# Two Toeplitz products summed in DRAM by the storing DMA, and a gate that loads and transposes one tensor instead of two

## The chip, the core and the metric

The kernel runs on one core of one Trainium2 chip. The core has five engines with queues of their own: TensorE (PE in the profile; its weight loads are shown apart as PEld), VectorE (DVE), ScalarE (ACT), GpSimd (POOL) and SyncE (SP), which here only issues transfers. Transfers issued by SP and by GpSimd run on the same 16 DMA engines. On-chip memory is SBUF (128 partitions) and PSUM ([...]into which TensorE writes its products); DRAM holds everything that doesn't fit. The metric is the time of one execution on the device, in microseconds (us).

## The reference, cut to what matters

The model is four layers on x of shape (8, 56, 56, 192): a Toeplitz gate, window attention, a depthwise convolution and a four-direction selective scan, with group or layer norms and residual sums between them. The change concerns the first layer only:

```python
p = silu(x @ p_w.T + p_b)                      # 576 channels
q = silu(x @ q_w.T + q_b)
v = silu(x @ v_w.T + v_b)
qv = q * v
o1 = toeplitz(qv along w, a1)                  # for every row h: a 56 x 56 Toeplitz matrix per channel
o2 = toeplitz(qv along h, a2)                  # for every column w: another one per channel
out = (p * (o1 + o2)) @ o_w.T + o_b
```

`a1` and `a2` come from small networks over the positions, once for all images. The sum `o1 + o2` is formed for each of 8 x 3136 tokens and 576 channels, all in float32.

## The kernel before, in words

**Order of the stages.** A first stage makes `qv` of images 0 to 3 (`products`) and writes it to DRAM as `qv_d[b][block]`, six blocks of 96 channels, tokens in rows of 96 values (384 bytes). The second makes both Toeplitz products of those images (`toeplitz`). Then the front of image 0 (gate, attention, convolution, inner projections, step sizes) runs step by step beside `products` and `toeplitz` of images 4 to 7. Last comes the scan loop over 5376 steps ("pairs": a chunk of 448 tokens, 128 channels and two states), 672 an image; into it the front of the next image is woven by a planner.

**`toeplitz`.** For each axis (the variable `ax`; 0 is the product along h, 1 the one along w) and each block of 96 channels: eight loads of 588 KB (two halves `u` of the other direction x four images) bring `qv` into `x` (tile `tzx`, L261), with 56 partitions for the position in the sequence in each half, and the other direction and the channels in the free one. On axis 0 a partition is a row h, and its 28 tokens of an image lie in one run of 28 x 384 bytes in DRAM; on axis 1 a partition is a column w, and each run has 384 bytes. Then for each of four groups of 24 channels, two loads (L270) place a Toeplitz matrix for each channel twice on the diagonal of `tm` (three buffers), TensorE makes one 112 x 112 x 112 product a channel (L274; each float32 product leaves two records in the profile), and VectorE and ScalarE copy four channels at a time from PSUM back over `x` (L280; VectorE alone in the second run). At the end of a block, eight stores on GpSimd's queue (L288) write `x` to `o_d[ax][b]`. Axis 1 is stored in the order (w, h), which makes its runs long; so the two products lie in DRAM in different token orders. `x` has three buffers in the first run and two in the second.

**The gate** (`gate`, one image): for each of seven chunks of 448 tokens, six projections (L467) with their bias (L471), one SiLU over them all (L473), then for each of six channel blocks one PSUM bank (L484): four groups of 112 tokens, and in each two products with the identity matrix, of the product along h and of that along w, that turn tokens x channels into channels x tokens and add the two in PSUM. VectorE multiplies `p` by the bank (L492). Two output products of six each follow (L497), a residual sum (L503) and statistics (L504). `load_ot` fetches two blocks at a time, one step ahead: for each block one load of the product along h (L444) and two of that along w (L450), which put its tokens back into the order (h, w); six transfers in all.

**What sets the order.** Every engine takes its queue in the order of the program. In the scan loop a step is: GpSimd fills the ring (L1007), ScalarE the decays (L1024), VectorE scans (L1033), GpSimd or VectorE in turn multiplies by C (L1039, tile `hc`, four buffers), TensorE sums with identity products (L1054). Between the steps, the planner (`Parts`) places pieces of the next image's front. A piece ends at each `yield`; `Meter` prices the pieces while the front of image 0 is emitted (0.04 us + 1.25 ns an element for a product), and a piece is placed when by these prices it fits into the engines' spare time. A front holds at most two PSUM banks (`ps`). In the second stage, pieces of `products` and `toeplitz` of images 4 to 7 are drawn after each piece of the front, 1.0 of the planner's us for every four channels, in the ratio of 0.55 to the price of the front's piece.

Of the kernel before, what the change touches and what calls it, by code (L numbers as in the profile page):

```python
# [15 lines left out]
F32 = mybir.dt.float32  # L16
AF = mybir.ActivationFunctionType
ALU = mybir.AluOpType
# [4 lines left out]
H = W = 56  # L23
L = H * W
C = 192
CP = 96
D1 = 576
CH = 448
NCH = L // CH
TT = 112  # L30
# [54 lines left out]
def model(ctx: ExitStack, tc: tile.TileContext, a: dict, out: bass.AP):  # L85
    nc = tc.nc
    B = out.shape[0]
# [8 lines left out]
    ident = load_const(const, "ident")  # L96
# [6 lines left out]
    ext = [dram.tile([D1 // TC, TT, TC], F32, name=f"ext{i}") for i in range(2)]  # L103

    qv_d = [dram.tile([D1 // CP, L, CP], F32, name=f"qv{b}") for b in range(B)]
    o_d = [[dram.tile([D1 // CP, L, CP], F32, name=f"o{i}_{b}") for b in range(B)] for i in range(2)]
    x1_d, x2_d, x3_d = ([dram.tile([C, L], F32, name=f"x{i}_{b}") for b in range(B)] for i in (1, 2, 3))
    z_d = [dram.tile([128, ND, L], F32, name=f"z{b}") for b in range(B)]
    zr_d = [dram.tile([128, ND, L], F32, name=f"zr{b}") for b in range(B)]
# [129 lines left out]
    def toeplitz(images, beside):  # L239
        G = len(images) * (H // 2)  # L240
        with (
            tc.tile_pool(name="tz", bufs=2) as sp,
            tc.tile_pool(name="tz_t", bufs=1) as tp,
            tc.tile_pool(name="tz_ps", bufs=4 if beside else 8, space=PSUM) as ps,
        ):

            tm = [tp.tile([TT, TT, TC], F32, name=f"tm{i}") for i in range(3)]
            for t in tm:
                nc.gpsimd.memset(t, 0.0)
            n_t = 0  # L250
            for ax in range(2):
                along_h = "(h u w) c -> u h w c"
                along_w = "(u h w) c -> u w h c"
                stored = "(w u h) c -> u w h c"
                size = dict(h=H, u=2) if ax == 0 else dict(w=W, u=2)
                for c0 in range(D1 // CP):
                    x = sp.tile([TT, G, CP], F32, name="tzx", bufs=2 if beside else 3)
                    for n, b in enumerate(images):
                        v = qv_d[b][c0].rearrange(along_w if ax else along_h, **size)
                        for u in range(2):  # L260
                            nc.sync.dma_start(out=x[u * W : (u + 1) * W, n * 28 : (n + 1) * 28, :], in_=v[u])  # L261
                    for c1 in range(0, CP, TC):
                        t = tm[n_t % 3]
                        n_t += 1
                        e = ext[1 - ax][(c0 * CP + c1) // TC]

                        src = bass.AP(e.tensor, e.offset, [[TC, W], [1, W * TC]])
                        for u in range(2):
                            dst = t[u * W : (u + 1) * W, u * W : (u + 1) * W, :].rearrange("p i c -> p (i c)")
                            nc.sync.dma_start(out=dst, in_=src)  # L270
                        for c2 in range(0, TC, 4):
# [8 lines left out]
                            copy(  # L280
                                x[:, :, cs].rearrange("p (b g) c -> p b g c", g=28)[:, :, ::-1, :],
                                po.rearrange("p c (b g) -> p b g c", g=28),
                            )
                            yield 1.0
                    for n, b in enumerate(images):
                        v = o_d[ax][b][c0].rearrange(stored if ax else along_h, **size)
                        for u in range(2):
                            nc.gpsimd.dma_start(out=v[1 - u], in_=x[u * W : (u + 1) * W, n * 28 : (n + 1) * 28, :])  # L288


    now, later = range(min(4, B)), range(min(4, B), B)
# [5 lines left out]
    with (  # L297
# [17 lines left out]
        def carve(base, parts, *shapes):  # L315

            views, at = [], 0
            for shape in shapes:
                n = 1
                for m in shape:  # L320
                    n *= m
                v = base[:parts, at : at + n]
                if len(shape) > 1:
                    names = [f"a{i}" for i in range(len(shape))]
                    v = v.rearrange(
                        f"p ({' '.join(names)}) -> p {' '.join(names)}", **dict(zip(names[1:], shape[1:]))
                    )
# [101 lines left out]

        def gate(b):  # L430

            w_p, w_o, x, s, ot = carve(slab, TT, (2, D1), (6, C), (2, 2, CH), (6, CH), (2, 2, 4, C))
# [21 lines left out]

            load_x(0)
            load_ot(0)
# [2 lines left out]
            for j in range(NCH):  # L459
# [15 lines left out]
                for c in range(6):  # L475
                    n = 3 * j + c // 2
                    if c % 2 == 0 and n + 1 < 3 * NCH:
                        load_ot(n + 1)
                    yield 0, 1

                    p = bank()
                    for t in range(4):
                        for i in range(2):
                            nc.tensor.matmul(  # L484
                                p[:CP, t * TT : (t + 1) * TT],
                                ot[:, n % 2, i, t, c % 2 * CP : c % 2 * CP + CP],
                                ident[:TT, :TT],
                                start=i == 0,
                                stop=i == 1,
                            )  # L490
                    yield 1, 0
                    nc.vector.tensor_mul(s[:, c, :], s[:, c, :], p[:CP, :CH])  # L492
                for m in range(2):
# [876 lines left out]
```

## Time and profile before

Three runs took 21826.98, 21839.35 and 21850.64 us; the median is 21839.35. The profiled execution took 21800.17 us, with a span of 21798.4 us from its first to its last instruction and a mean granted TensorE clock of 0.888.

| engine | busy us | share of the span |
|---|---|---|
| TensorE | 18274.4 | 84% |
| VectorE | 15858.5 | 73% |
| GpSimd | 15084.9 | 69% |
| ScalarE | 12098.2 | 56% |

| what (line) | count | busy us | mean of one |
|---|---|---|---|
| Toeplitz products (L274), records | 4608 | 1031.5 | 403 ns |
| gate's identity products (L484), records in the scan loop | 4704 | 522.4 | 265 ns |
| attention's transposes (L647), records in the scan loop | 1344 | 336.5 | 326 ns |
| gate's multiplication (L492) in the scan loop | 294 | 177.2 | 603 ns |
| product stores (L288) issued by GpSimd | 192 | 97.3 | 513 ns |
| gate's loads of the product along h (L444), 168 KB each | 336 | | |
| gate's loads of the product along w (L450), 84 KB each | 672 | | |

A share is an average over stages with different limits, so the stretch that an edit touches has to be looked at by itself. Records of one operation overlap: TensorE's 403 ns is from start to end, while the next one starts sooner. The span falls into `products` (to 505 us), `toeplitz` of images 0 to 3 (505 to 1120), the front of image 0 beside the products of images 4 to 7 (to about 3355), and the scan loop. In the first front, whose instructions were emitted through the pricing helper, lines of the front appear as L79.

### The profile page before, as it was taken

Reading aid. Unit: us, or ns where it says so; the run is one execution under the profiler, and the core shown is the slowest. Engines: PE = TensorE matmul, PEld = TensorE weight load, DVE = VectorE, ACT = ScalarE, POOL = GpSimd, SP = SyncE. Lnnn points to the kernel's source line nnn. Section 1 sums busy time; section 2 is a strip of 40 time slices with the busy share of each in tenths; the row PEclk is TensorE's granted clock in tenths of the full one; section 3 lists DMA queues with packets and bytes.
Section 4 is the critical chain, followed back from the end, with each engine's and each line's share of the span. In section 5 each row is a group of like instructions: output and inputs, shape, how many; then the busy total and the mean of one; then the engine's idle time right before and its main releaser. Section 6 shows DMA issues by size and latency. Waiting matters only on the chain. (4 is left out here: it accounts for less than half of the span.)

```text
span 21798.4 us, 194536 instructions
## 1 busy us (share of the span) xinstructions
PE 18274.4 (84%) x58396; PEld 9706.4 (45%) x58396; DVE 15858.5 (73%) x12604; ACT 12098.2 (56%) x28153; POOL 15084.9 (69%) x9175
## 2 busy tenths in 40 slices
PE   7978977888888989888888889888988888887777
PEld 4845654444443434444444434443444444343333
DVE  2122117996799768986799769976898589976998
ACT  3126114655666466755666566746675566656555
POOL 0000006887789778977788768976898678877998
PEclk9588868999999989998999989998999899998888
DMA  3931575444544455445644455345544464445443
GB/s 86 245 98 49 170 196 169 126 135 159 187 143 135 136 184 170 129 129 171 184 133 136 154 184 150 123 150 170 169 129 140 156 185 132 135 155 175 134 138 116
DMA packets 2419572, 3249.82 MB, mean 149 GB/s; under 512 B 917598, under 2 KB 2361024, under 8 KB 2387554
## 3 DMA queue, kind: packets, MB, share of 16 engines
q1 hardware_dynamic: 2398292, 3121.12, 47.5%
q0 software_dynamic: 15520, 116.14, 1.4%
q8 instruction: 463, 7.59, 0.1%
q14 instruction: 593, 4.86, 0.1%
q10 hardware_dynamic: 4704, 0.12, 0.0%
HBM read 2661.35 MB, written 575.48 MB: 148 GB/s over the span
## 5 line engine op out<-in xcount | busy, mean ns | idle before, releaser
L1007 POOL TENSOR_TENSOR ring<-du,bm 128x896 f32<-128x896 f32 x5376 | 9447.8, 1771 | 1983.9 <-ACT ring L1014 1937.8
L1054 PE MATMUL ps_y<-hc,ident_sb 128*128 128x448 f32 x21504 | 9818.6, 591 | 590.2 <-POOL hc L1039 573.3
L1024 ACT ACTIVATE ps_a<-delta,A_logs_sb 128x449 f32<-128x449 f32 x10752 | 6858.4, 638 | 331.5 <-DVE ring L1033 68.7
L1054 PEld LDWEIGHTS ps_y<-hc,ident_sb 128*128 128x128 f32 x21504 | 4271.5, 207 | 4640.8 <-issue 3494.9
L1033 DVE TENSOR_TENSOR_SCAN ps_a<-ps_a,ring 128x898 f32<-128x898 f32 x2688 | 5429.0, 2020 | 1062.5 <-ACT ring L1014 555.0
L1033 DVE TENSOR_TENSOR_SCAN ring<-ps_a,ring 128x898 f32<-128x898 f32 x2688 | 5423.0, 2017 | 420.4 <-ACT state L1046 177.3
L1039 POOL TENSOR_TENSOR hc<-ring,cm 128x896 f32<-128x896 f32 x2688 | 4758.0, 1770 | 860.9 <-DVE ring L1033 349.3
L1039 DVE TENSOR_TENSOR hc<-ps_a,cm 128x896 f32<-128x896 f32 x2688 | 2935.0, 1092 | 974.5 <-PE ps_y L1054 753.3
L1046 ACT COPY state<-ps_a 128x2 f32<-128x2 f32 x2687 | 425.3, 158 | 3254.0 <-DVE hc L1039 3250.0
L280 DVE COPY tzx<-ps_tz 112x448 f32<-112x448 f32 x432 | 269.8, 625 | 1389.9 <-PE ps_tz L274 1175.0
L274 PE MATMUL ps_tz<-tzx,tm 112*112 112x112 f32 x4608 | 1031.5, 403 | 257.6 <-DMA tm<-ext 233.0
L288 POOL DMA_DIRECT2D o<-tzx x192 | 97.3, 513 | 1653.6 <-DVE tzx L280 1318.7
L274 PEld LDWEIGHTS ps_tz<-tzx,tm 112*112 112x112 f32 x4608 | 1028.0, 319 | 295.2 <-issue 288.7
L817 PE MATMUL ps_f<-slab 128*128 128x448 f32 x2646 | 1086.4, 546 | 69.9 <-DMA slab<-dg_d 62.1
L1046 ACT COPY state<-ring 128x2 f32<-128x2 f32 x2688 | 504.9, 188 | 791.3 <-DVE ring L1033 778.4
L647 PE MATMUL ps_f<-ident_sb,slab 98*98 98x98 f32 x1344 | 336.5, 326 | 619.6 <-ACT slab L640 619.6
L749 PE MATMUL ps_f<-slab 96*96 96x448 f32 x1764 | 725.1, 547 | 47.7 <-DVE slab L736 47.7
L817 PEld LDWEIGHTS ps_f<-slab 128*128 128x128 f32 x2646 | 506.8, 192 | 560.5 <-issue 485.0
L79 PE MATMUL ps_f<-slab 96*96 96x448 f32 (+6 forms) x2306 | 731.2, 497 | 10.2 <-DMA slab<-x 4.9
L990 POOL TENSOR_TENSOR du<-delta,xcd 128x448 f32<-128x448 f32 x672 | 658.6, 980 | 23.6 <-DMA xcd<-xc 23.6
L647 PEld LDWEIGHTS ps_f<-ident_sb,slab 98*98 98x98 f32 x1344 | 203.9, 158 | 1033.7 <-ACT slab L640 814.6
L227 PE MATMUL ps_qv<-wqv,xn 96*128 96x384 f32 (+1 forms) x1200 | 527.0, 522 | 128.2 <-DVE xn L146 67.5
(218 smaller groups left out, 17070.7 us busy)
## 6 DMA issues: line engine op xcount, KB each, us to landing
bm<-bc SPq DMA_DIRECT2D x1792, 448.0 KB
cm<-bc SPq DMA_DIRECT2D x1792, 448.0 KB
xcd<-xc SPq DMA_DIRECT2D x840, 224.0 KB
dl<-slab SPq DMA_DIRECT2D x224, 672.0 KB
delta<-dl SPq DMA_DIRECT2D x224, 672.0 KB
tzx<-qv SPq DMA_DIRECT2D x192, 588.0 KB
o<-tzx POOLq DMA_DIRECT2D x192, 588.0 KB, 13.7
slab<-x SPq DMA_DIRECT2D x224, 336.0 KB
```

What stands on the lines that cost most here:

```text
L79: return f(*args, **kw)
L274: nc.tensor.matmul(po[:, c, :], t[:, :, c2 + c], x[:, :, c1 + c2 + c], start=True, stop=True)
L647: nc.tensor.transpose(p[:PT_, e * PT_ : (e + 1) * PT_], S[:, 3 * g + e, :], ident[:PT_, :PT_])
L749: nc.tensor.matmul(p[:CP, :CH], dg[:, k, t, :], xp[:, u, k, dy : dy + 8, dx : dx + W], start=t == 0, stop=t == 8,)
L817: nc.tensor.matmul(p[:, :CH], dg[:, t, :], xp[:, 8 * j + dy : 8 * j + dy + 8, dx : dx + W], start=t == 0, stop=t == 8,)
L990: nc.gpsimd.tensor_mul(du[:, 0, :], deltas[i][:, d, 1 : CH + 1], xcs.pop((i, d)))
L1007: nc.gpsimd.tensor_mul(hs[:, :, tokens(i)[0]], dus[i, d].to_broadcast([128, NG, CH]), bms[i, k])
L1024: nc.scalar.activation(dA[:, n, :], deltas[i][:, d, at : at + CH + 1], AF.Exp, scale=negA[:, slot, d, c : c + 1])
L1033: nc.vector.tensor_tensor_scan(h, dA, hs, 0.0, ALU.mult, ALU.add)
L1039: (nc.gpsimd if on_pool(d, k) else nc.vector).tensor_mul(hc, h[:, :, tokens(i)[0]], cms[i, k])
L1046: nc.scalar.copy(states[i][:, d, NG * k : NG * k + NG], h[:, :, tokens(i)[2]])
L1054: nc.tensor.matmul(yps[i, d][:, :CH], ident, hcs[g][:, n, :], start=k + n == 0, stop=k + n == NP + NG - 2)
```

## The change

One DRAM tensor `o_d[b]` for each image takes the place of two. `toeplitz` goes through axis 1 (along w) first and stores its product plainly, in token order, by eight transfers a block on SP's queue; each now writes runs of 384 bytes. Axis 0 (along h) follows, and its stores, on GpSimd's queue, add to what is in DRAM (`accum_op`); each is cut in two along its 28 columns, so there are sixteen of 294 KB a block. A block's stores are issued later than before: `held` keeps them until the next block's loads of `x` and of its first Toeplitz matrix have been issued. The gate loads one tensor, two transfers for two blocks instead of six, and turns each group of 112 tokens with one `transpose` instead of two identity products that add.

```diff
-    o_d = [[dram.tile([D1 // CP, L, CP], F32, name=f"o{i}_{b}") for b in range(B)] for i in range(2)]
+    o_d = [dram.tile([D1 // CP, L, CP], F32, name=f"o{b}") for b in range(B)]
...
+            def store():
+                ax, c0, x = held
+                for n, b in enumerate(images):
+                    v = o_d[b][c0].rearrange(along_w if ax else along_h, **sizes[ax])
+                    for u in range(2):
+                        xu = x[u * W : (u + 1) * W, n * 28 : (n + 1) * 28, :]
+                        if ax:
+                            nc.sync.dma_start(out=v[1 - u], in_=xu)
+                            continue
+                        for g in range(0, 28, 14):
+                            nc.gpsimd.dma_start(
+                                out=v[1 - u][:, g : g + 14], in_=xu[:, g : g + 14], accum_op=ALU.add
+                            )
+
-            for ax in range(2):
+            for ax in (1, 0):
                 along_h = "(h u w) c -> u h w c"
                 along_w = "(u h w) c -> u w h c"
-                stored = "(w u h) c -> u w h c"
...
                         for u in range(2):
                             dst = t[u * W : (u + 1) * W, u * W : (u + 1) * W, :].rearrange("p i c -> p (i c)")
                             nc.sync.dma_start(out=dst, in_=src)
+                        if held:
+                            store()
+                            held = None
...
-                    for n, b in enumerate(images):
-                        v = o_d[ax][b][c0].rearrange(stored if ax else along_h, **size)
-                        for u in range(2):
-                            nc.gpsimd.dma_start(out=v[1 - u], in_=x[u * W : (u + 1) * W, n * 28 : (n + 1) * 28, :])
+                    held = ax, c0, x
+            store()
...
                     nc.sync.dma_start(
-                        out=ot[:, n % 2, 0, :, to],
-                        in_=o_d[0][b][blk, j * CH : (j + 1) * CH, :].rearrange("(t p) c -> p t c", p=TT),
+                        out=ot[:, n % 2, :, to],
+                        in_=o_d[b][blk, j * CH : (j + 1) * CH, :].rearrange("(t p) c -> p t c", p=TT),
                     )
-                    v = o_d[1][b][blk].rearrange("(w h) c -> h w c", h=H)
-                    for r in range(2):
-                        nc.sync.dma_start(
-                            out=ot[r * W : (r + 1) * W, n % 2, 1, :, to],
-                            in_=v[8 * j + r : 8 * j + 8 : 2].rearrange("t w c -> w t c"),
-                        )
...
                     for t in range(4):
-                        for i in range(2):
-                            nc.tensor.matmul(
-                                p[:CP, t * TT : (t + 1) * TT],
-                                ot[:, n % 2, i, t, c % 2 * CP : c % 2 * CP + CP],
-                                ident[:TT, :TT],
-                                start=i == 0,
-                                stop=i == 1,
-                            )
+                        nc.tensor.transpose(
+                            p[:CP, t * TT : (t + 1) * TT],
+                            ot[:, n % 2, t, c % 2 * CP : c % 2 * CP + CP],
+                            ident[:TT, :TT],
+                        )
```

More of the change, by code (lines that the diff above doesn't have):

```diff
@@ L249, in toeplitz @@
                 nc.gpsimd.memset(t, 0.0)
-            n_t = 0
-            for ax in range(2):
+            n_t, held = 0, None
+            def store():
[12 more added lines that the diff above has]
+            for ax in (1, 0):
                 along_h = "(h u w) c -> u h w c"
                 along_w = "(u h w) c -> u w h c"
-                stored = "(w u h) c -> u w h c"
-                size = dict(h=H, u=2) if ax == 0 else dict(w=W, u=2)
+                sizes = dict(h=H, u=2), dict(w=W, u=2)
                 for c0 in range(D1 // CP):
@@ L258, in toeplitz @@
                     for n, b in enumerate(images):
-                        v = qv_d[b][c0].rearrange(along_w if ax else along_h, **size)
+                        v = qv_d[b][c0].rearrange(along_w if ax else along_h, **sizes[ax])
                         for u in range(2):
@@ L430, in gate @@
         def gate(b):
-            w_p, w_o, x, s, ot = carve(slab, TT, (2, D1), (6, C), (2, 2, CH), (6, CH), (2, 2, 4, C))
+            w_p, w_o, x, s, ot = carve(slab, TT, (2, D1), (6, C), (2, 2, CH), (6, CH), (2, 4, C))
             w_p, w_o, x, s = w_p[:CP], w_o[:CP], x[:CP], s[:CP]
```

## The prediction

> **What bounds the kernel now.** I first read the busy time of each engine by stage (columns: stretch in us, its length, then busy us and instruction counts of TensorE, its weight loads, VectorE, ScalarE and GpSimd; last the granted TensorE clock, the DMA share and GB/s).
>
> ```profile
> 505.00:1120.00 615.00, 510.42 (x2304) 507.83 (x2304) 90.12 (x146) 76.61 (x144) 55.96 (x100) 0.50 0.87 236
> 1120.00:2190.00 1070.00, 890.58 (x3601) 516.00 (x3602) 272.79 (x544) 480.16 (x1212) 15.85 (x8) 0.83 0.29 71
> 2190.00:3355.00 1165.00, 947.54 (x3350) 713.59 (x3348) 205.28 (x336) 173.07 (x218) 50.66 (x97) 0.72 0.64 181
> 3355.00:20000.00 16645.00, 14200.11 (x45058) 7136.06 (x45059) 13546.19 (x10324) 10245.86 (x24091) 13243.56 (x7937) 0.92 0.50 153
> 20000.00:21798.00 1798.00, 1305.56 (x2810) 591.48 (x2808) 1609.81 (x1024) 955.41 (x2160) 1705.07 (x1026) 0.87 0.40 132
> ```
>
> The change touches the first Toeplitz stage (505 to 1120), which stands alone; the second (2190 to 3355), beside the first image's front; and the gate, which recurs in seven stretches of the scan loop. The order of time shows GpSimd issuing the product stores once per channel block:
>
> ```profile
> 622.99 4.05 POOL L288 DMA_DIRECT2D o<-tzx  x8 [40.87 <-DVE tzx L280]
> 668.32 2.54 POOL L288 DMA_DIRECT2D o<-tzx  x5 [41.27 <-DVE tzx L280]
> ...
> 901.17 4.05 POOL L288 DMA_DIRECT2D o<-tzx  x8 [45.58 <-DMA tm<-ext]
> 949.86 4.05 POOL L288 DMA_DIRECT2D o<-tzx  x8 [44.63 <-DMA tm<-ext]
> ```
>
> A block takes 45 us on axis 0 and 49 us on axis 1; TensorE needs 192 records at 0.22 us (427 in 94.5 us), 42.6 us. The rest is transfer. Short stretches of the same columns, each filled by one kind, give its rate: 384-byte stores of qv; loads along h; stores with Toeplitz loads; loads along w; stores alone.
>
> ```profile
> 452.00:456.00 4.00, 4.00 (x14) 2.39 (x13) 0.76 (x1) 1.47 (x3) 0.00 (x0) 1.00 0.77 198
> 525.00:530.00 5.00, 0.00 (x0) 0.00 (x0) 0.00 (x0) 0.00 (x0) 0.00 (x0) 0.50 0.86 196
> 910.00:915.00 5.00, 5.00 (x24) 5.00 (x24) 1.25 (x2) 0.53 (x1) 0.00 (x0) 0.50 0.89 377
> 940.00:945.00 5.00, 5.00 (x25) 5.00 (x25) 0.62 (x1) 0.96 (x2) 0.00 (x0) 0.50 1.17 176
> 1110.00:1115.00 5.00, 0.00 (x0) 0.00 (x0) 0.00 (x0) 0.00 (x0) 0.00 (x0) 0.50 0.87 348
> ```
>
> One block loads 8 x 588 KB (4.82 MB), stores as much, and loads 8 x 294 KB (2.41 MB) of Toeplitz matrices. At these rates (191 GB/s along h and 170 along w, taken over neighbouring stretches): load along h 25.2 us, along w 28.3, store 13.8, matrices 6.9. Axis 0 sums to 45.9 and axis 1 to 49.0, the pitches seen: both axes are bound by transfers, TensorE close behind.
>
> The gate stretches (5828 to 6236 is one) hold seven chunks of some 57.3 us. TensorE is busy 386 of 408 us, so the gate looks TensorE-bound; the order of time says where it is not.
>
> ```profile
> 6026.42 1.70 PE L484 MATMUL ps_f<-ident_sb,slab 112*96 112x112 f32 x16
> 6027.96 1.68 PE L1054 MATMUL ps_y<-hc,ident_sb 128*128 128x448 f32 x4
> 6031.32 1.77 PE L484 MATMUL ps_f<-ident_sb,slab 112*96 112x112 f32 x16 [1.68 <-DVE slab L492]
> ...
> 6042.96 1.68 PE L1054 MATMUL ps_y<-hc,ident_sb 128*128 128x448 f32 x4
> 6044.53 2.47 PE L497 MATMUL ps_f<-slab 96*96 96x448 f32 x6
> ```
>
> ```profile
> 6043.77 0.61 DVE L492 TENSOR_TENSOR slab<-slab,ps_f 96x448 f32<-96x448 f32 x1
> ```
>
> L497 starts 0.15 us after the fifth L492 (6044.38), which frees its bank. I compared these two in all 49 chunks: 33 have that gap, to 0.01 us. VectorE has no gap from 6027.5 to there: it is VectorE that sets this part, and TensorE the L497 and L467 parts. The other 16 are 0.9 to 5.2 us late (57 us in all); those I followed begin with a late load:
>
> ```profile
> 6214.08 0.66 PE L484 MATMUL ps_f<-ident_sb,slab 112*96 112x112 f32 x2 [5.13 <-DMA slab<-o]
> ```
>
> Summing how far each chunk exceeds 57.3 us gives 76 us over the loop.
>
> [...] Nothing before shows an adding store. [...] The attention's transposes show its price here:
>
> ```profile
> 3871.30 0.83 PE L647 MATMUL ps_f<-ident_sb,slab 98*98 98x98 f32 x3 [1.81 <-ACT slab L640]
> 3871.97 1.69 PE L1054 MATMUL ps_y<-hc,ident_sb 128*128 128x448 f32 x4
> ```
>
> Three take 0.67 us, 0.22 each[...]. A gate bank costs 16 records x 94 ns = 1.5 us now and 4 x 0.22 = 0.9 after.
>
> **The change part by part**, against the profiled 21800.2 us (span 21798.4).
>
> *Axis 1's stores* become 384-byte runs and move from GpSimd's queue to SP's. The qv stores made 198 GB/s at share 0.77, so 257 at 1[...]. Bounds: 13.8 (no loss) to 28.3 (the rate of loads along w). I take 21.4: +7.6 x 6 = **+46** in the first stage. On SP the eight stores are issued after the next block's x loads and its first matrix; SP waits there for the block's last eviction, and the second matrix queues behind the data. TensorE idles some 11 us after the first 24 products, ends at 22 + 32 = 54 us, inside the transfer-bound 56.6, so this adds nothing more.
>
> *Axis 0's stores* become adding ones, 16 of 294 KB a block on GpSimd. [...] Bounds: 13.8[...] to 55 (four times). I take 27.6: 59.7 us a block, **+83** for six, the exposed last one included. GpSimd's own issue, 16 x 0.51 us, is hidden by its idleness there. Loading along w first: **+3**.
>
> *Second stage.* The same 46 + 83 + 3 are added to blocks that last 75 to 100 us, paced by the front. Blocks along w now come first, where TensorE is 90% busy and the DMA share 0.5 to 0.65: most is covered, but SP's wait for evictions keeps the front's loads behind it; 5 us x 6 = 30. Adding stores fall on the tail (share 0.71 to 0.79; TensorE waited 101 us for matrices): half exposed, 41. Loads there gain 3 x 6 us, half of it: -9, and the last adding store delays the scan's buffers by 3 more. **+65**, between -10 and +150.
>
> *Gate.* First image: 42 banks x 0.6 = 25 us of TensorE where it is 90 to 100% busy: **-20**. Scan loop: the built order puts every front piece beside the same scan steps as before (125 steps a gate, all seven), so only durations count. 49 chunks x 6 x 0.6 = 176 us of TensorE are saved, but where VectorE is last: nothing by itself. Loads fall from six per pair of blocks to two, half the bytes: of the 76 us lost to lateness I take 60. Against it, TensorE idles 2.9 instead of 1.7 us before the third bank[...]: +15. **-45**, between -90 and +30.
>
> Sum: 46 + 83 + 3 + 65 - 20 - 45 = **+132**, 21932 on the profiled run. The median of the runs shown, 21839, stands 39 above it, so **21970**.
>
> **Rivals.**
>
> *The adding store is dear* (four times a plain one[...]). Nothing in the profile prices it. 27.6 us more x 6 in the first stage, 60% of it in the second: +166 + 100, 22236. Chance 0.2.
>
> *The adding store costs a plain one*: -83 - 41, 21846. For it: while stores and matrices run, 377 GB/s pass, and loads reach only 190[...]. Chance 0.18.
>
> *The gate is TensorE-bound after all* (the other side). If L492 comes earlier once the banks are filled earlier, all 176 us show, and the 76 with them: -252 for -45, 21763. For it: TensorE's 95% in the gate. Against: the 0.15 us in 33 of 49. It turns the sign when the loop gains over 177 us, 3.6 us of each chunk's 57.3; it is faster by a measurable amount from 221. Chance 0.12.
>
> [...]
>
> **How the numbers follow.** 0.5 for the forecast, whose own range is 21880 to 22080. About 0.2%, 44 us, is what a measurement of this kernel can tell from no change. Faster: 0.12 and a fifth of 0.18, 0.15. Same: half of 0.18 and a little of the forecast, 0.12. Slower: 0.73. The range, 21790 to 22240, reaches to the dear store and almost to the gate rival: about 0.1 below and 0.08 above.
>
> **What would show it.** The issue times of the stores give a pitch near 57 us for axis 1 and 60 for axis 0, and the first stage ends near 1250. A pitch of 46 on axis 0 says the plain price, one over 70 the dear one. In the gate, L484 shows four records a bank, L497 still 0.15 us after the fifth L492, chunks of 57.3 us, and few waits for the products. Chunks of 54 us or less would make the forecast wrong, as would a second stage that still takes 1165 us.

## The result: 0.34% slower, 21912.7 us for 21831.8

Six runs of the changed kernel took 21897.87 to 21921.08 us, median 21912.71; six of the kernel before, beside them, 21807.58 to 21850.64, median 21831.76. The ratio is 1.0034, with a 95% interval of 1.0023 to 1.0045. A second measurement on another chip gave 1.0034 again (1.0021 to 1.0046). The medians of the kernel before differ from one measurement to the next (21832 to 21851), so what follows compares ratios of runs made side by side, or stages within traces.

The profiled execution took 21915.94 us (span 21914.1) for 21800.17 (span 21798.4). The difference of the two spans, 116 us, is larger than that of the medians, 81, as the profiled execution of the kernel before is faster than every other run of it on record (the next takes 21807.58). Where the 116 us lie, from three marks in each trace (the clearing of the Toeplitz buffers at the start of each Toeplitz stage, GpSimd's clearing of `bias` after the first one, and the first scan):

| stretch | before | after | difference |
|---|---|---|---|
| to the first Toeplitz stage | 505.4 | 502.2 | -3.2 |
| first Toeplitz stage, with its last stores | 624.5 | 744.0 | +119.5 |
| first front beside the products and Toeplitz work of images 4 to 7 | 2274.0 | 2306.5 | +32.5 |
| scan loop | 18394.6 | 18361.3 | -33.3 |

The 119.5 stand against a short first stage: the Toeplitz code of the kernel before takes 620 to 666 us in four traces (see the first experiment).

The busy times by stage, after (columns as in the prediction: stretch, length, busy us and counts of TensorE, weight loads, VectorE, ScalarE, GpSimd; granted clock, DMA share, GB/s):

```profile
502.00:1237.00 735.00, 512.52 (x2304) 508.34 (x2304) 90.12 (x146) 76.65 (x144) 87.40 (x100) 0.50 0.89 197
1237.00:2355.00 1118.00, 939.71 (x3371) 510.02 (x3372) 294.75 (x588) 493.18 (x1232) 11.09 (x5) 0.84 0.26 67
2355.00:3553.00 1198.00, 845.93 (x3077) 666.59 (x3075) 181.19 (x293) 164.72 (x204) 96.28 (x108) 0.66 0.73 182
3553.00:20000.00 16447.00, 13855.31 (x41296) 6782.85 (x41298) 13449.44 (x10266) 10151.74 (x23921) 13150.18 (x7875) 0.91 0.48 149
```

In the first Toeplitz stage TensorE's busy time is what it was (512.5 for 510.4), over 735 us for 615; the DMA engines are as busy (0.89 for 0.87) but move 197 GB/s for 236. The same bytes (145 MB, length times rate) take longer to pass, with engines that show as busy as before. The order of time (start, us over the group, queue or engine, line) has one block of axis 1 on SP's queue, and the stores of two blocks of axis 0:

```profile
643.71 21.64 SPq L259 DMA_DIRECT2D o<-tzx  x8
665.45 5.70 SPq L284 DMA_DIRECT2D tm<-ext  x6
671.20 26.70 SPq L275 DMA_DIRECT2D tzx<-qv  x8
697.99 4.15 SPq L284 DMA_DIRECT2D tm<-ext  x2
706.56 21.69 SPq L259 DMA_DIRECT2D o<-tzx  x8
...
1053.52 6.78 POOL L262 DMA_DIRECT2D o<-tzx  x8 [29.36 <-DVE tzx L297]
1103.34 6.77 POOL L262 DMA_DIRECT2D o<-tzx  x8 [25.64 <-DVE tzx L297]
```

In that block of 62.9 us SP issues for 58.2 and waits 4.4 to start the next stores. The first store takes 0.3 us to issue, the later ones 1.6 to 4.1, with a median of 3.0 over the eight; from 656 to 664 us 177 to 211 GB/s pass, at which 588 KB take 2.9 to 3.4 us, so SP seems to issue these stores at the pace of the transfers. Axis 1 now takes 62.6 us a block (581.10 to 956.94 for six) for 49.8 before, and axis 0 49.2 (956.94 to 1203.15 for five) for 44.6. What TensorE waits for in that stage, first after, then before (us in total, times, longest):

```profile
PE ps_tz L291 <- DMA tm<-ext: 193.8, 17, 42.1
```

```profile
PE ps_tz L274 <- DMA tm<-ext: 89.4, 11, 35.4
```

One chunk of the gate after, TensorE's order of time and then VectorE's fifth multiplication:

```profile
6164.91 0.55 PE L492 MATMUL ps_f<-ident_sb,slab 112*96 112x112 f32 x4
6165.30 3.19 PE L1060 MATMUL ps_y<-hc,ident_sb 128*128 128x448 f32 x8
...
6174.41 0.95 PE L492 MATMUL ps_f<-ident_sb,slab 112*96 112x112 f32 x4 [4.02 <-issue]
6175.16 2.78 PE L1060 MATMUL ps_y<-hc,ident_sb 128*128 128x448 f32 x4
...
6187.60 2.47 PE L503 MATMUL ps_f<-slab 96*96 96x448 f32 x6 [1.64 <-DVE slab L498]
```

```profile
6186.85 0.61 DVE L498 TENSOR_TENSOR slab<-slab,ps_f 96x448 f32<-96x448 f32 x1
```

A bank is four records in 0.55 us for sixteen in 1.7. TensorE idles before the third bank and before the output products instead, and L503 starts 0.14 us after the end (6187.46) of the fifth L498, as before. What has gone is the waiting for the products, over the scan loop before and after:

```profile
PE ps_f L484 <- DMA slab<-o: 40.9, 27, 5.1
```

```profile
PE ps_f L492 <- DMA slab<-o: 5.6, 4, 1.7
```

### The profile page after: what moved, and what is told of

Same layout as the page of the kernel before. It is cut to its first block, busy times and chain, and to the rows that moved or that the text cites. A ratio compares the mean times of both kernels' runs of the same rounds, so it can differ in the third digit from the quotient of the medians.

```text
span 21914.1 us, 185052 instructions
## 1 busy us (share of the span) xinstructions
PE 17979.6 (82%) x54364; PEld 9343.4 (43%) x54364; DVE 15850.9 (72%) x12604; ACT 12103.5 (55%) x28154; POOL 15156.4 (69%) x9175
## 5 line engine op out<-in xcount | busy, mean ns | idle before, releaser
L262 POOL DMA_DIRECT2D o<-tzx x192 | 160.2, 1402 | 1705.5 <-DVE tzx L297 1109.1
```

## The experiments

The theory ahead of them: the first stage pays for axis 1's short runs and for SP's order more than for the adding; the loop's gain comes from loads that arrive in time, not from the transposes. A name such as "first stage" means the stretches of the table above; "front and second stage" is its third row.

### How far a stage can be read: the changed kernel again

No edit.

> The changed kernel once more, unaltered, for a time and a trace from the same chip as the runs beside it. Theory: what differs between two traces of it tells how far a stage's time can be read: first Toeplitz stage 744 us from its first to the end of its last store within 5 us, scan loop 18361 us within 30; against the kernel before 1.003 to 1.004. Rival (its first trace is unlike the others): the stages ahead of the scan loop, 3552.8 us there, come out 40 us or more shorter.

Ratio 1.0034 (1.0021 to 1.0046). First stage 748.5 us, front and second stage 2302.6, loop 18354.2. The changed kernel's stages ahead of the loop repeat within 5 us. Those of the kernel before do not: its Toeplitz code takes 624.5 us in its own trace, and 619.7, 649.1 and 665.5 in three traces of kernels below that leave it as it is ("Loads in time without the sum", "The mirror of it", "The new gate alone"). In the two longer ones some blocks on axis 1 take 57 to 72 us for 49 to 51. The two with the short stage are the fastest runs of their kernels on record, 21800.17 and 21777.61 us, so a usual run of the kernel before may well have the longer one; then up to 41 of the 119.5 us are not the change's, which would also explain 116 us between the spans for 81 between the medians. Only one run of the kernel before was traced, so that isn't shown.

The loop is less steady too: over the eleven traces of kernels here whose gate loads one tensor it takes 18345 to 18386 us, mean 18368.

### What the adding costs

```diff
                             nc.gpsimd.dma_start(
-                                out=v[1 - u][:, g : g + 14], in_=xu[:, g : g + 14], accum_op=ALU.add
+                                out=v[1 - u][:, g : g + 14], in_=xu[:, g : g + 14]
                             )
```

> The changed kernel with plain instead of adding stores; everything else stays. The product along h then overwrites that along w, so the sum of the two is left out[...]. Against the changed kernel: first Toeplitz stage 734.5 us, axis-0 pitch 50.0 us, second Toeplitz stage 1197 us. Theory (the add costs transfer time, about 0.4 of a plain store): the pitch of axis 0 falls from 50.0 to about 45, the first stage by some 30 us, the second by 10 to 40, the whole by 50 us. Rival 1 (the add costs next to nothing, and the held, cut stores make the pitch): pitch 49 to 50, the whole within 15 us of the changed kernel. Rival 2 ([...]part of it is hidden in the changed kernel): the whole falls by over 80 us, as the second stage gains 50 or more.

Ratio to the kernel before 1.0003 (0.9996 to 1.0010), so 0.31%, 68 us, under the changed kernel; 56 to 60 us by the traces' spans. First stage 717.8 us, 26 to 31 shorter; front and second stage 2254.3, 48 to 52 shorter. Two of its blocks on axis 0:

```profile
1055.13 4.03 POOL L262 DMA_DIRECT2D o<-tzx  x8 [32.95 <-DVE tzx L297]
1099.02 4.03 POOL L262 DMA_DIRECT2D o<-tzx  x8 [29.83 <-DVE tzx L297]
```

The pitch, over five blocks, is 45.4 us for 49.2. The add costs 3.8 us a block in the first stage, where the prediction had 13.8. The last adding stores, with nothing beside them, take 33.6 us from their first issue to GpSimd's next work (1203.15 to 1236.73) for 20.9 (1191.13 to 1212.04). Two windows within these, the adding ones first, then the plain ones (columns as above), show that the rate then falls to little over half:

```profile
1212.00:1230.00 18.00, 0.00 (x0) 0.00 (x0) 0.00 (x0) 0.00 (x0) 5.09 (x7) 0.50 0.92 174
```

```profile
1195.00:1205.00 10.00, 0.00 (x0) 0.00 (x0) 0.00 (x0) 0.00 (x0) 4.17 (x9) 0.50 0.87 300
```

By itself an adding store is as dear as predicted: 4.82 MB at 174 GB/s are 27.7 us, for the 27.6 taken. Beside loads of `x` and of matrices, most of that does not lengthen the block. GpSimd takes 0.50 us to issue one of these and 0.85 us for an adding one (6.77 for eight), which stays hidden. The first stage went as the theory had it. In the second the add is worth some 50 us, more than its upper bound of 40. From the front's last product to the first scan (the tail of the experiments with the old price) it takes 170 us for 188, so 18 of the 50 lie there and the rest beside the front; what they meet there wasn't taken apart.

### Short runs, or SP's queue

Three kernels take the two properties of axis 1's new stores apart. Long runs, still on SP:

```diff
-                    v = o_d[b][c0].rearrange(along_w if ax else along_h, **sizes[ax])
+                    v = o_d[b][c0].rearrange(stored if ax else along_h, **sizes[ax])
...
                 along_w = "(u h w) c -> u w h c"
+                stored = "(w u h) c -> u w h c"
```

> The changed kernel with the product along w stored in the order (w, h), in long runs, still on SP's queue and still held. The product along h is then added to tokens in another order, so the sum is that of the wrong tokens; every transfer has the same size. Theory (the runs of 384 bytes are the larger part of what axis 1 costs): axis-1 pitch falls from 62.6 us to 51 to 54, the first stage by 50 to 70 us, the whole by 60 to 90. Rival (SP's order is what costs: matrices and loads queue behind stores that wait for the last eviction): the pitch stays at 58 or more, the first stage falls by at most 28 us.

Short runs on GpSimd's queue, at the same place of the program:

```diff
-                            nc.sync.dma_start(out=v[1 - u], in_=xu)
+                            nc.gpsimd.dma_start(out=v[1 - u], in_=xu)
```

> The changed kernel with the product along w stored from GpSimd's queue instead of SP's, at the same place of the program (held), in the same runs of 384 bytes. Theory (runs of 384 bytes set the transfer time; SP's order adds the idle part only): axis-1 pitch 56 to 58 us for 62.6, the first stage 28 to 40 us shorter, the second up to 30 us shorter. Rival (SP's order is what costs): pitch 49 to 52, the first stage 65 us or more shorter, and the second some 50 shorter, as the front's loads no longer wait behind the stores.

And the same at the end of the block:

```diff
                     held = ax, c0, x
+                    if ax:
+                        store()
+                        held = None
```

> As the kernel that stores the product along w from GpSimd's queue, but at the end of the block, not held until the next block's loads have been issued; a full computation. Theory: GpSimd waits for the evictions alone, so the place in the program makes no difference: pitch within 1.5 us of the held one, the whole within 15 us of it, and so still slower than the kernel before (first stage 690 to 710 us for 614 before). Rival (the held place delays the stores): pitch 3 us or more below the held one.

Six blocks of axis 1, from the first store of axis 1 to the first of axis 0 (for the kernel before, from the last block's store of axis 0 to the last of axis 1, six blocks too):

| axis 1's stores | long runs | runs of 384 bytes |
|---|---|---|
| GpSimd's queue | 298.8 us (before); 298.0, 326.0, 336.1 in other traces of its Toeplitz code | 350.7 held, 350.3 at the end |
| SP's queue, held | 338.0 | 375.8, 378.6 (the changed kernel, twice) |

Seen from the changed kernel, whose corner is steady, long runs save 38 to 41 us and GpSimd's queue 25 to 28. Against the trace of the kernel before, short runs alone cost 52 us, SP's queue alone 39, both 77 to 80. As that corner lies between 298 and 336, these three are the upper ends of 14 to 52, 2 to 40 and 40 to 80. So what the record supports is the view from the changed kernel: each property, taken back alone, saves time, the runs more than the queue.

Neither answer of the long-run experiment was right about the pitch: it is 56.3 us, between the two; and the first stage, 702.5 us, is 42 to 46 shorter, under the theory's 50 to 70. Its ratio is 0.9997 (0.9988 to 1.0006), 81 us below the changed kernel, as the theory had it, since front and second stage (2265.8 us) also lose 37 to 41. On GpSimd the pitch is 58.4 on the mean, near the theory's 56 to 58 and far from the rival's 50, and the place in the program makes no difference: ratios 1.0006 (0.9997 to 1.0014) held and 1.0007 (1.0001 to 1.0014) at the end. The held one's first stage, 719.8 us, is 24 to 29 shorter, less than the theory had, its front and second stage, 2268.9, 34 to 38, more than it had. The stores with long runs on SP, for the 21.64 us above:

```profile
637.09 11.77 SPq L259 DMA_DIRECT2D o<-tzx  x8
693.94 11.81 SPq L259 DMA_DIRECT2D o<-tzx  x8
```

On GpSimd the mean hides a beat: blocks of 49 and 75 us in turn. The windows of the held one show why (columns as above):

```profile
649.00:654.00 5.00, 0.00 (x0) 0.00 (x0) 0.00 (x0) 0.00 (x0) 0.00 (x0) 0.50 1.01 240
669.00:674.00 5.00, 5.00 (x25) 5.00 (x24) 1.25 (x2) 0.53 (x1) 0.00 (x0) 0.50 0.00 0
```

and TensorE's order of time there:

```profile
665.86 42.56 PE L291 MATMUL ps_tz<-tzx,tm 112*112 112x112 f32 x192 [32.28 <-DMA tm<-ext]
```

First TensorE has nothing to do for 32 us, until the block's first matrix has come; it was issued after the loads, and in the first window the DMA share is 1.01, at 240 GB/s. Then the DMA engines have nothing to do (share 0.00): SP's next loads stand behind matrices whose buffers TensorE has yet to free. These blocks are bound by transfers and by TensorE in turn, not by one of them.

### Loads or transposes: the gate with two products

```diff
-                        nc.tensor.transpose(
-                            p[:CP, t * TT : (t + 1) * TT],
-                            ot[:, n % 2, t, c % 2 * CP : c % 2 * CP + CP],
-                            ident[:TT, :TT],
-                        )
+                        for i in range(2):
+                            nc.tensor.matmul(
+                                p[:CP, t * TT : (t + 1) * TT],
+                                ot[:, n % 2, t, c % 2 * CP : c % 2 * CP + CP],
+                                ident[:TT, :TT],
+                                start=i == 0,
+                                stop=i == 1,
+                            )
```

> The changed kernel with the gate's bank made as before, by two adding identity products for each group of 112 tokens, both of the one loaded tensor (the product counts twice in the gate, so the output is another one). TensorE has the work of the kernel before in the gate, the transfers those of the changed kernel. Theory (VectorE sets this part of a chunk; the scan loop's gain is that of fewer and shorter loads): chunks of 56.4 and 57.3 us stay, the scan loop within 25 us of the changed kernel's (18345 to 18386 us over five traces of it and its variants), only the first front 10 to 30 us longer. Rival (the gate is TensorE-bound): 6 x 0.6 us more in each of 49 chunks, the loop 120 to 176 us longer.

The scan loop went as the theory had it: 18377.8 us, and the chunks of 56.4 and 57.3 us stay. The sum of 36 distances from chunk to chunk (six in each of the last six gates) is 2110.5 us in the kernel before, 2066.3 in the changed one and 2067.1 here, with all of the old TensorE work (the changed kernel's second trace has 2058.9). The waits for the products here:

```profile
PE ps_f L493 <- DMA slab<-o: 8.2, 9, 1.6
```

The first front went against both answers. With more TensorE work this kernel is faster: ratio 1.0011 (1.0005 to 1.0018), 48 us under the changed kernel on the same chip. The gain is in front and second stage, 2251.8 us for 2302.6 to 2306.5. Something other than TensorE's time was in the transposes. The pricing helper, too, sees four instructions where there were eight.

### The new gate alone

In the kernel before, the gate takes one tensor and transposes; both Toeplitz stages are the old ones.

```diff
-                    v = o_d[1][b][blk].rearrange("(w h) c -> h w c", h=H)
-                    for r in range(2):
-                        nc.sync.dma_start(
-                            out=ot[r * W : (r + 1) * W, n % 2, 1, :, to],
-                            in_=v[8 * j + r : 8 * j + 8 : 2].rearrange("t w c -> w t c"),
-                        )
...
-                        for i in range(2):
-                            nc.tensor.matmul(
...
+                        nc.tensor.transpose(
```

> The kernel before with the changed gate alone: it loads only the product along h, and turns it by transposes. The product along w is computed and stored but left out of the sum. Both Toeplitz stages stay as before. Theory (what the new gate gains is 20 us in the first front and some 30 in the loop, by fewer late loads): first stage 614 us as before, front and second stage together 2255 us for 2274, loop 18345 to 18386 for 18394.6, the whole some 45 us faster than before, ratio 0.998. Rival (the new gate's loop gains nothing, and the loop's difference lies between traces): ratio 0.9995 to 1.0005.

Ratio 0.9965 (0.9953 to 0.9978), 75 us faster, where the theory had 45. Front and second stage take 2242.6 us for 2274.0, the loop 18374.6. Its first stage shows 665.5 us with the Toeplitz code of the kernel before, 41 more than there, with blocks of 48 to 71 us on axis 1, for example:

```profile
876.70 4.05 POOL L288 DMA_DIRECT2D o<-tzx  x8 [67.33 <-DVE tzx L280]
```

Why the same code fell into that beat in this trace wasn't followed; the trace was the slowest of its five runs. The new gate is worth 75 us where the sum costs nothing; on the same chip the changed kernel, which adds the new Toeplitz stages to it, takes 148 us more (21923.9 for 21775.8).

### The draw: the transposes at the old price

While the first front is emitted, each of its pieces draws products and Toeplitz work beside it for 0.55 of its price. The gate's price fell by 42 x 4 x (0.04 + 112 x 0.00125), 30 us, so 17 us of pieces are drawn later. In the built order 200 Toeplitz products stand behind the front's last step sizes, for 144 before: call this the tail, in which nothing of the front runs. Here each of the gate's transposes counts twice in the helper, and the instructions stay:

```diff
+            if name == "transpose" and n == TT:
+                base, each = 2 * base, 2 * each
```

> The changed kernel, a full computation, in which the pricing helper counts each of the gate's transposes twice, so that the first front's gate draws as many pieces of the products and Toeplitz work beside it as in the kernel before; the instructions are the same, only their order in the first front differs. Theory (the new gate's lower price moves 42 x 0.72 x 0.55 = 17 pieces, 0.7 of a block, from beside the front to the tail behind it, and so the second stage pays what the transposes save): the second Toeplitz stage starts some 60 us earlier (near 2295 us for 2355 and 2362), the time from the front's end to the scan loop falls from 188 to about 150 us, front and second stage together from 2303 to 2306 to 2235 to 2260, the whole 45 to 70 us faster than the changed kernel, ratio to the kernel before 1.000 to 1.0012. Rival (the kernel with two identity products gained by its position against the transfers, not by the draw): front and second stage together stay above 2285, ratio 1.002 or more.

Ratio 0.9990 (0.9982 to 0.9998): 0.44%, 96 us under the changed kernel, and more than the theory had. Front and second stage take 2208.5 us. The tail is 150 us for 188, as expected; in addition the front itself ends 60 us sooner (3304 us for 3364), and the second Toeplitz stage starts at 2243 us, 50 earlier than expected. TensorE's waits for matrices from the first stage's end to the first scan, in the changed kernel and here:

```profile
PE ps_tz L291 <- DMA tm<-ext: 178.3, 10, 31.7
```

```profile
PE ps_tz L294 <- DMA tm<-ext: 47.6, 5, 16.9
```

In the changed kernel the draw thus decides how often a matrix is late (153.6 us in its second trace); it presumably does so by which parts of the front stand beside which Toeplitz blocks, which no run tests. In the kernel before the old price doesn't prevent these waits: 143.5 us there. The tail of the kernel before, of the changed one and of this, in TensorE's order of time:

```profile
3247.76 1.86 PE L79 MATMUL ps_f<-slab,w_dt_sb 12*128 12x448 f32 x4
3249.55 21.46 PE L274 MATMUL ps_tz<-tzx,tm 112*112 112x112 f32 x96
3303.73 42.56 PE L274 MATMUL ps_tz<-tzx,tm 112*112 112x112 f32 x192 [32.71 <-DMA tm<-ext]
```

```profile
3362.65 1.86 PE L79 MATMUL ps_f<-slab,w_dt_sb 12*128 12x448 f32 x2
3364.44 3.86 PE L291 MATMUL ps_tz<-tzx,tm 112*112 112x112 f32 x16
3396.74 42.56 PE L291 MATMUL ps_tz<-tzx,tm 112*112 112x112 f32 x192 [28.44 <-DMA tm<-ext]
3446.05 42.56 PE L291 MATMUL ps_tz<-tzx,tm 112*112 112x112 f32 x192 [6.76 <-DMA tm<-ext]
```

```profile
3302.08 1.86 PE L82 MATMUL ps_f<-slab,w_dt_sb 12*128 12x448 f32 x4
3308.05 21.44 PE L294 MATMUL ps_tz<-tzx,tm 112*112 112x112 f32 x96 [4.10 <-DMA tm<-ext]
3346.43 42.56 PE L294 MATMUL ps_tz<-tzx,tm 112*112 112x112 f32 x192 [16.94 <-DMA tm<-ext]
```

288 records (144 products) are left behind the front before and here, 400 (200 products) in the changed kernel.

The mirror of it, in the kernel before: the gate's identity products at half their price.

```diff
+            if name == "matmul" and n == TT:
+                base, each = base / 2, each / 2
```

> The kernel before, a full computation, in which the pricing helper counts the gate's identity products at half, so that the first front draws as few pieces beside it as in the changed kernel; the instructions are the same, only their order in the first front differs: 200 instead of 144 Toeplitz products of the second stage stand behind the front's last step sizes. Theory (the draw costs time by itself): the tail from the front's end to the scan loop grows from 154 to 185 to 195 us, front and second stage together from 2271 to 2274 to 2295 to 2345, ratio 1.001 to 1.003. Rival (the draw matters only with the new stores): front and second stage within 12 us of 2273, ratio 0.9994 to 1.0006.

Ratio 1.0013 (1.0006 to 1.0019). The tail grows from 154 to 192 us, front and second stage to 2299.2: the draw costs 25 us in the kernel before too. The trace also has 25 us more in the first stage, with the beat of the first experiment, and 32 in the loop, which the edit doesn't explain: in the loop it moves 35 of the gates' banks by one step, and the chunks' distances stay as before (2113.4 us for 2110.5).

### Both repairs

The old price, with axis 1 stored from GpSimd's queue in both stages:

> As the kernel with the old price, and with the product along w stored from GpSimd's queue at the end of each block; a full computation. Theory (the two repairs add up, as one acts on the transfers' order and the other on the draw): 59 to 62 us faster than the changed kernel by the queue and 45 to 70 by the price, of which both shorten the same waits for matrices in the second stage, so 80 to 115 together: ratio 0.9985 to 0.9998, at or a little below the kernel before. Rival (they remove the same waits): no faster than the better of the two, ratio 1.0004 or more.

Ratio 0.9997 (0.9988 to 1.0005): the first stage gains 18 us (724.4 for 742.3), front and second stage lose 39 (2247.6 for 2208.5). With the old draw, SP's order is the better one in the second stage; TensorE waits 115.6 us for matrices there, for 47.6. The ratio lies in the theory's range, but the rival was right that the two don't add up: it is slower than with the old price alone, 21849.4 us for 21826.6. So each stage got its own queue:

```diff
-                            nc.gpsimd.dma_start(out=v[1 - u], in_=xu)
+                            (nc.sync if beside else nc.gpsimd).dma_start(out=v[1 - u], in_=xu)
...
-                    if ax:
+                    if ax and not beside:
                         store()
```

> The kernel with the old price, with the product along w stored from GpSimd's queue at the end of each block in the first Toeplitz stage, and from SP's queue, held, in the second; a full computation. Theory (each stage for itself: GpSimd's queue gains some 20 us in the first stage, and SP's order was better in the second once the draw was the old one, front and second stage 2208 us together for 2248): the first stage 720 to 725 us for 742, front and second stage within 15 us of 2208, the whole some 20 us under the kernel with the old price, ratio to the kernel before 0.9975 to 0.9987. Rival (what the second stage takes depends on how its transfers happen to fall, and an earlier start changes it by tens of us): front and second stage outside 2190 to 2230, ratio 0.999 or more.

Ratio 0.9978 (0.9969 to 0.9988), 21800.7 us for 21843.9: first stage 721.5, front and second stage 2207.7, as the theory had it. This is the changed kernel with two small repairs: 0.22% faster than the kernel before, and 0.56% faster than the changed one.

### Loads in time without the sum

The kernel before, with the same transfers into four places of one block each, issued three blocks ahead:

```diff
-                    if c % 2 == 0 and n + 1 < 3 * NCH:
-                        load_ot(n + 1)
+                    if n + 3 < 6 * NCH:
+                        load_ot(n + 3)
```

> The kernel before, with the gate's loads of the two products kept in four places of one channel block each in place of two places of two, and issued three blocks ahead; the same transfers, the same work, a full computation. Theory (the loop's gain in the changed kernel is that of loads that come in time, so loads issued earlier bring the most of it without the new sum): the chunks of 59 to 65 us that wait for a load of the products (11 of 36 periods over 58.5 us) go down to 5 or fewer, the loop 20 to 45 us shorter, ratio 0.998 to 0.999, and so faster than both kernels. Rival (the loads are late because the transfers of a chunk are too many, three a block on one queue): as many late chunks as before, ratio 0.9995 to 1.0005.

Ratio 0.9982 (0.9975 to 0.9989), 46 us faster. Of the 36 distances 3 are over 58.5 us, for 11, their sum is 2072.8 us for 2110.5, and the waits for the products fall from 40.9 us to 10.9. The loop of the trace is 13 us shorter, less than expected, within the 41 us by which loops differ from trace to trace. Of the 44 us that the chunks gain in the changed kernel, 38 are to be had by loading earlier, without the sum in DRAM.

## Why the prediction was right, and where not

It gave 21970, within 21790 to 22240, and 73% for slower; 21912.7 was measured, 57 less. On traces its sum was +132, and +116 came out: that is 16 of the 57. The rest is the 39 us by which the median of the kernel before stands above its traced run. The prediction carried them over, but the changed kernel's traced run stands 3 us above its median. Direction and size were right; that the sum comes so near is in part luck, as several terms were wrong and cancelled. Step by step:

**Axis 1's stores, +46: the step that moved them to SP was wrong.** The stretch came out 77 us longer than in the trace of before. The 21.4 us a block for short runs agree with the 21.6 that SP takes over the eight stores; that they cost 46 by themselves is within what the GpSimd kernels allow (14 to 52). The prediction let TensorE end at 54 us "inside the transfer-bound 56.6" and added nothing for SP's order. It costs 25 to 28 us more on top of the short runs. The pitch was 62.6, not 56.6: SP issues for 58.2 us in the block shown, and then stands still for 4.4 us, until it can start the next stores. That this wait and the late matrices are the whole of the 25 to 28 us is argued from the traces, not tested by itself. The 21.4 was the author's estimate, 257 GB/s at a share near 0.87; the prediction's lines from 525, 910 and 1110 us have shares of 0.86 to 0.89, but nothing shows that this is a limit: its line from 940 us has 1.17.

**Axis 0's adding stores, +83: too dear.** Axis 0 and the end of its last block came out 36 us longer, of which plain stores save 26 to 31. The 27.6 us for 13.8, a factor of two, were the author's estimate; no trace before has an adding store. For one that has the engines to itself it is nearly right here (174 GB/s for 300). What failed is the sum of transfers one after the other: beside loads and matrices a block of axis 0 takes 49.2 us for 45.4, little over a quarter of the 13.8 us taken. The **+3** for loading along w first is 6: the first store comes 78.9 us after the stage's start for 72.6. The first stage's 132 became 120 as a dear term and a missing one nearly cancelled, which is luck; and if the longer first stage is the usual one of the kernel before, the 120 are 80 to 95.

**Second stage +65 and first gate -20: the sum near (+45, measured +29 to +33), the terms not.** The prediction's step held the work beside the front fixed. The draw had to be in it: with the old price restored, front and second stage fall from between 2302.6 and 2306.5 us to 2208.5, so the lower price of the gate cost 94 to 98 us. Against that, the transposes, at the old price, save 43 us there (2251.8 with two products, 2208.5), twice the 20; and the new Toeplitz stage with the gate's loads is 22 us below the kernel before (2251.8 for 2274.0), where +65 was taken. Three wrong terms made a right sum. How much of the 94 to 98 us is tail (38) and how much the changed meeting of transfers (60) is seen in the traces; which transfer holds up which matrix wasn't taken apart further.

**Scan loop, -45: right in its reasons.** VectorE sets the L498 part: with the old TensorE work the 36 distances sum to 2067.1 us, for 2066.3 and 2058.9 in two traces of the changed kernel. The gain is that of late loads, 44 us in those 36, some 52 in the seven gates' 42, for the 60 taken. The loop as a whole is 27 us shorter on the mean of eleven traces than in the one trace of the kernel before; as two other traces with its gate's transfers have 18381.9 and 18426.5 us for its 18394.6, that figure is rough. The +15 was the author's estimate of what a lower TensorE clock costs. The clock is lower: the mean granted clock of the profiled run is 0.878 to 0.882 in every kernel with transposes, 0.885 to 0.888 in every one with identity products. Whether the transposes do this, or the smaller work of TensorE, was not told apart, and what it costs was not measured. One statement was inexact: by the new price 35 of the gates' 294 banks do stand one step earlier in TensorE's queue in the loop.

**The rivals.** The dear store is out (an add costs a quarter of a plain store's time in the first stage, not three times it). The cheap store was nearer than the forecast for the first stage, and what spoke for it, 377 GB/s with stores and matrices for 190 with loads, fits the pitch of 49.2 us for 45.4; in the second stage, where the add costs some 50 us, it was not. The TensorE-bound gate is out by the kernel with two products.

## What to carry to other kernels

An edit that shortens work also changes what a price-driven planner does with everything around it: compare the built order where the planner draws as well as where it places, and hold the price fixed in an experiment before judging the edit. A store moved to the queue that issues loads puts its wait, and the time of its issue, ahead of them (here 4.4 and 21.6 us of a block of 62.9): add up that queue's time for a block before trusting the sum of the transfers. A transfer that is slower by itself (here 174 GB/s for 300) need not lengthen a block by as much: 3.8 us here, for the 13.8 predicted. When a gain comes from transfers that arrive in time, first try to issue them earlier (here for 38 of 44 us). And trace the kernel before more than once: the same code had two lengths of one stage here, some 620 us and 649 to 666.

## What the runs showed of the hardware

- DRAM stores that add pass 174 GB/s with nothing beside them, plain ones of the same size 300; the last block's took 33.6 us from the first issue to GpSimd's release for 20.9. Where the engines also serve loads, the add lengthened a block of 4.82 MB by 3.8 us only (49.2 for 45.4); in the second stage it was 48 to 52 us for six blocks, the front beside them included.
- GpSimd's issue of one store took 0.50 us plain and 0.85 us adding (both 294 KB), 0.51 us plain with 588 KB in long runs, and 1.04 us (8.34 for eight) with 588 KB in runs of 384 bytes: not the bytes alone set it.
- A bank of four float32 transposes, 112 x 96 each, took 0.55 us where eight identity products took 1.7. With the transposes, and the smaller work, the mean granted clock of the whole program was 0.879, for 0.885 in the changed kernel with two products.
